# Linear attention through the tokens' Gram matrix instead of keys and values, in a four-layer image network

## The chip, the cores and the metric

The kernel runs on one core of one Trainium2 chip. The metric is the device time of one execution in microseconds; for the kernel before, it is the median of three runs, 8629.55 us (8617.16 to 8655.84). A change of about half a per cent, 43 us, is what such runs can tell from none.

An execution of the kernel before was also recorded by the profiler. Its records name five engines: PE (TensorE, with PEld for its weight loads), DVE (VectorE), ACT (ScalarE), POOL (GpSimd) and SP (SyncE, which here only issues transfers).

## The reference

The input is x of shape (4, 96, 64, 64): four images of 96 channels and 4096 pixels. Four layers follow each other:

- Layer 0: group normalization, a projection, a depthwise convolution and a selective state-space scan in four directions over the 4096 pixels, with a gate and an output projection.
- Layer 1: group normalization and a deformable 3 by 3 convolution (each output pixel gathers nine interpolated input pixels).
- Layer 2: over tokens, a Fourier mixing block, then a feed-forward net in 8-bit arithmetic.
- Layer 3: linear attention, then a second feed-forward net.

The change concerns only the attention. Without its residual it is

```python
qkv = x @ Wqkv + bqkv
q, k, v = jnp.split(qkv, 3, axis=-1)
attn = jnp.einsum('bhnd,bhmd->bhnm', q, k) * D ** (-0.5)
y = jnp.einsum('bhnm,bhmd->bhnd', attn, v)
return y.reshape(B, N, E) @ Wff + bff
```

with 6 heads of 16 channels and x normalized per token (the transposes that move the heads are left out here). There is no softmax, so the order of the products is free: for each head, the sum over all tokens of k times v transposed is a 16 by 16 matrix, and everything behind it is one 97 by 96 matrix that is applied to the tokens.

Written with e, a token with a one appended (97 numbers), keys are Wk'e and values Wv'e, biases included. The sum over tokens of v k' is Wv' (sum of e e') Wk. The sum in brackets is the 97 by 97 Gram matrix of the tokens.

## The kernel before

The whole network is one program. What is placed when is not left to a compiler: a planner writes the instructions of every engine in one order, which each engine then keeps (`in_program_order`).

Three streams of work are merged:

- the scan of layer 0 (`Layer0.scan`), 1536 units of 128 lanes by 1024 steps; it sets the pace;
- the stream `ends`: what comes before the scan for the four images, and layers 2 and 3 (`Layers23.image`), one image after the other;
- the stream `middle`: what follows the scan of an image (`Layer0.behind`), and layer 1 (`Layer1.image`).

Work is written as generators that yield steps with their costs (`cost(pe=..., act=...)`, in us as the planner assumes them). `Clock` keeps the time at which each engine would be free; `has_room` lets a step in if its input is ready and its engines aren't too far ahead of the scan. `pipe` runs several chains of steps side by side, at most `width` at a time, and takes the oldest one that may go. After each scan unit both streams are asked for steps until neither has one that fits; `middle` is asked first (`ends` first in the last image's sampling). So the costs that a step states decide where its instructions and all those after it stand.

`Layers23.image` waits until layer 1 has sampled the image, loads its 96 by 4096 tokens (`t`) by a transfer on SP's queue, and runs the Fourier block, the first feed-forward net, the attention and the second net on it. For the last image nothing is left to lie beside: it is split into two halves of 2048 tokens that run as two streams, with a meeting in the attention, where the sums of both halves are added.

The attention is `LinearAttention.run`. First `normed` makes `tl`, the normalized tokens with a 97th row of ones, channels on partitions (lines 1725 to 1727): `centred` subtracts the mean and gathers the variances, and `spread` (L527) repeats the inverse deviations over partitions. Then come

- `keys_and_values(m)`, for each block of 128 tokens: a matmul of the block with the key and value weights into PSUM (`pk`, L1734), a copy to SBUF by ACT (`kv`, L1736), and a matmul that adds values times keys to `pa` (L1738), three blocks at a time in `pipe` (L1743);
- the product of `pa` with the mask of heads, `vk` (L1748), and for the last image the addition of both halves (L1755);
- two small matmuls with a copy each, `p1` with the output weights (L1759, L1761) and `p2` with the query weights (L1764, L1766), which give the matrix `m2`;
- for each chunk of 512 tokens a matmul with `m2` (`p3`, L1775) and the addition to `t` (L1777).

PSUM is short: the scan has banks of its own, and all other work shares three of them (`net.mm`) until the scan is over; then the stream `ends` gets five more. `net.hold(1)` reserves the one in which `pa` is summed.

Three other places matter for the prediction. L1034 multiplies the scan's input `db`, which PE has spread by L1020, and L1042 scans it. L1295 and L1297 in layer 1 transpose four blocks of 128 pixels on PE and copy them to SBUF. L1112 loads `yta` and `ytc`, layer 0's column results, for `behind`.

Of the kernel before, what the change touches and what calls it, by code (L numbers as in the profile page):

```python
# [8 lines left out]
F32 = mybir.dt.float32  # L9
# [10 lines left out]
B, C, H, W = 4, 96, 64, 64  # L20
# [162 lines left out]
def cost(pe=0.0, dve=0.0, act=0.0, pool=0.0, **more):  # L183
    return Step((pe, dve, act, pool), **more)


def wait(us=0.0, **more):

    return Step((0.0,) * 4, us, **more)
# [82 lines left out]
def pipe(net, chains, width, every=0, lane=None, **tiles):  # L272


    chains, active = iter(chains), []
    clock, known, more = net.clock, net.known, True
    end, free = clock.now(), tiles
    while True:
        if more and len(active) < width:
            steps = next(chains, None)  # L280
            if steps is None:
                more = False
            else:
                active.append(Chain(steps, clock.now()))
                continue
        if not active:
            break
        for n, chain in enumerate(active):
            if chain.new and not net.has_bank():
                continue  # L290
            if any(
                a.done <= chain.done + every
                for a in active[:n]
                if lane is None or (a.kind is lane) == (chain.kind is lane)
            ):
                continue
            if not all(free[tag] > 0 for tag in chain.takes):
                continue
            if clock.has_room(known.get((chain.kind, chain.done), (1.0,) * 4), chain.ready):
                break  # L300
        else:
            yield BLOCKED
            continue
        for tag in chain.takes:
            free[tag] -= 1
        clock.precede(known.get((chain.kind, chain.done), (0.0,) * 4))
        step = next(chain.steps, None)
        if step is None:
            net.hold(-chain.holds)
            active.remove(chain)  # L310
            end = max(end, chain.ready)
            continue
        for tag in step.frees:
            free[tag] += 1
        known[chain.kind, chain.done] = step.work
        chain.ready = clock.queue(step, chain.ready)
        chain.done += 1
        net.hold(step.holds - chain.holds)
        chain.holds, chain.new, chain.takes = step.holds, step.new, step.takes
        yield None  # L320
    yield wait(max(0.0, end - clock.now()))
# [1124 lines left out]
class Fourier:  # L1446
# [77 lines left out]
    def run(self, b, t):  # L1524

        net = self.net
        tc, nc = net.tc, net.nc
        with tc.tile_pool(name=f"l2b{b}", bufs=1) as big:
            tl = big.tile([C + 1, L], F32, name=f"tl{b}", tag="tl")
            nc.gpsimd.memset(tl[C:], 1.0)  # L1530
            with tc.tile_pool(name=f"l2n{b}", bufs=2) as pool:
                yield from normed(net, t, tl, f"2_{b}", pool)
            tv = tl.rearrange("c (n1 n2) -> c n1 n2", n2=64)
            with tc.tile_pool(name=f"l2s{b}", bufs=2) as pool:
                for g in range(2):
                    yield from self.half(f"{b}_{g}", g, tv, t, pool, pool)
# [66 lines left out]
def normed(net, t, tl, key, pool, groups=(0, 1)):  # L1603

    rs = yield from net.centred(
        t, net.cen96, lambda j: (tl[:C, j * CH : (j + 1) * CH], plain), key, pool, groups=groups
    )

    def chain(j):
        cs = slice(j * CH, (j + 1) * CH)  # L1610
        pb = net.spread(rs, 32 * (j % 4) + groups.index(j // 4), C, key)
        yield cost(pe=1.2, holds=1)
        net.nc.vector.tensor_mul(tl[:C, cs], tl[:C, cs], pb)
        yield cost(dve=0.7)

    yield from pipe(net, (chain(j) for j in chunks(groups)), 3)


def chunks(groups):
    return [4 * r + q for r in groups for q in range(4)]  # L1620
# [87 lines left out]
class LinearAttention:  # L1708
# [8 lines left out]
    def run(self, b, t, groups=(0, 1), side="left", shared=None):  # L1717
        net = self.net
        tc, nc = net.tc, net.nc
        key = f"{b}_{groups[0]}"  # L1720
        with (
            tc.tile_pool(name=f"l3b{key}", bufs=1, side=side) as big,
            tc.tile_pool(name=f"l3s{key}", bufs=2, side=side) as pool,
        ):
            tl = big.tile([C + 1, L], F32, name=f"tl3{key}", tag="tl")
            nc.gpsimd.memset(tl[C:], 1.0)
            yield from normed(net, t, tl, f"3_{key}", pool, groups)
            net.hold(1)
            pa = net.mm(f"pa{key}", C)[:, :C]
            blocks = [4 * j + i for j in chunks(groups) for i in range(4)]  # L1730

            def keys_and_values(m):
                pk = net.mm(f"pk{b}_{m}")[:, : 2 * C].rearrange("p (s c) -> p s c", c=C)
                nc.tensor.matmul(pk, lhsT=tl[:, 128 * m : 128 * m + 128], rhs=self.wkv, start=True, stop=True)  # L1734
                kv = pool.tile([128, 2, C], F32, name=f"kv{b}_{m}", tag="kv", bufs=3)
                nc.scalar.copy(kv, pk)  # L1736
                yield cost(pe=0.55, act=0.4)
                nc.tensor.matmul(  # L1738
                    pa, lhsT=kv[:, 1, :], rhs=kv[:, 0, :], start=(m == blocks[0]), stop=(m == blocks[-1])
                )  # L1740
                yield cost(pe=0.4)

            yield from pipe(self.net, (keys_and_values(m) for m in blocks), 3)  # L1743

            if shared is None:
                shared = {}
            vk = shared[groups[0]] = pool.tile([C, C], F32, name=f"vk{key}", tag="vk")
            nc.vector.tensor_mul(vk, pa, self.heads)  # L1748
            net.hold(-1)
            yield cost(dve=0.3)  # L1750
            if len(groups) == 1:
                while len(shared) < 2:
                    yield BLOCKED
                if groups[0] == 0:
                    nc.vector.tensor_add(vk, vk, shared[1])  # L1755
                    yield cost(dve=0.3)
            if groups[0] == 0:
                p1 = net.mm(f"p1{b}", C)[:, :128]
                nc.tensor.matmul(p1, lhsT=vk, rhs=self.wff, start=True, stop=True)  # L1759
                m1 = pool.tile([C, 128], F32, name=f"m1{b}", tag="m1")  # L1760
                nc.scalar.copy(m1, p1)  # L1761
                yield cost(pe=0.6, act=0.3)
                p2 = net.mm(f"p2{b}", C + 1)[:, :128]
                nc.tensor.matmul(p2, lhsT=self.wqT, rhs=m1, start=True, stop=True)  # L1764
                m2 = shared["m2"] = pool.tile([C + 1, 128], F32, name=f"m2{b}", tag="m2")
                nc.scalar.copy(m2, p2)  # L1766
                yield cost(pe=0.6, act=0.3)
            while "m2" not in shared:
                yield BLOCKED
            m2 = shared["m2"]  # L1770

            def chunk(j):
                cs = slice(j * CH, (j + 1) * CH)
                po = net.mm(f"p3{b}_{j}")
                nc.tensor.matmul(po, lhsT=m2, rhs=tl[:, cs], start=True, stop=True)  # L1775
                yield cost(pe=1.0, holds=1)
                nc.vector.scalar_tensor_tensor(t[:, cs], po[:C], net.vec(V_BFF, C), t[:, cs], ALU.add, ALU.add)  # L1777
                yield cost(dve=0.8)

            yield from pipe(self.net, (chunk(j) for j in chunks(groups)), 3)  # L1780
            shared[f"over{groups[0]}"] = True
            while len(groups) == 1 and not ("over0" in shared and "over1" in shared):
                yield BLOCKED
# [137 lines left out]
```

## Time and profile before

| | before |
|---|---|
| median of three runs | 8629.55 us |
| the profiled execution | 8600.48 us |
| its span, first to last instruction | 8598.7 us |
| mean granted clock of TensorE | 0.785 |
| PE busy | 6553.4 us (76%) |
| VectorE busy | 6817.9 us (79%) |
| ScalarE busy | 4945.4 us (58%) |
| GpSimd busy | 5626.7 us (65%) |
| scan of layer 0, first to last unit | 184.9 to 7550.5 us |
| sampling of the last image ends | 8171 us |

The attention's first stage in the four images, by the starts of the first `pk` and the first `vk`:

| image | from, us | to, us | what runs beside it |
|---|---|---|---|
| 0 | 5544.7 | 5642.4 | scan, `behind` |
| 1 | 6877.8 | 6981.6 | scan, sampling of image 2 |
| 2 | 7888.6 | 7929.9 | sampling of image 3 |
| 3 | 8496.4 | 8524.8 | the other half of image 3 |

In a line of the profile's groups stand the line of the program, the engine and operation, output and inputs by name, shapes and count; after the first bar the busy time and the mean duration of one in ns; after the second, how long the engine stood idle just before them and who ended most of that. Shares of busy time are means over stages with different limits. An fp32 matmul shows as two records. In the timeline, lines give start and duration in us, the engine, the line and operation, output from inputs, and in brackets the idle time before. The chain is the chain of work that ended last, followed back from the end. In the waits, each line names who waited, for whom, for how long in total, how often, and the longest.

### The profile page before, as it was taken

What the parts mean: (1) busy time and instruction counts of PE and PEld (TensorE: products, weight loads), DVE (VectorE), ACT (ScalarE), POOL (GpSimd) and SP (SyncE); (2) the same over time, 40 slices, a digit from 0 to 9 for tenths busy, and PEclk for the clock granted to TensorE, in tenths of its full rate; (3) what the DMA queues carried; (4) which work ended last, traced back from release to release, by engine and by line L of the source; (5) the groups of instructions that cost most, each with busy time, mean ns of one, the idle gap of its engine ahead of it and who ended that gap; (6) DMA issues with size and microseconds to landing.
All of it is one profiled execution on the core that took longest, in us unless ns stands there. A gap on an engine that the chain in (4) does not pass through costs nothing.

```text
span 8598.7 us, 97186 instructions
## 1 busy us (share of the span) xinstructions
PE 6553.4 (76%) x31960; PEld 2840.7 (33%) x31960; DVE 6817.9 (79%) x5118; ACT 4945.4 (58%) x9071; POOL 5626.7 (65%) x4308
## 2 busy tenths in 40 slices
PE   6775877689767668777767888777788776897587
PEld 2211221122222223311223555223455331464374
DVE  2799989888799888688898888888887887838714
ACT  5664666556567668755666667554567765333224
POOL 1565667566579788665688888665787886527700
PEclk8766877779677779876777888676788887798698
DMA  3677678868779889876888989766898887744420
GB/s 97 166 198 195 169 196 220 210 166 201 182 216 243 220 230 226 204 193 181 209 228 223 230 230 229 169 163 166 229 228 226 204 216 180 180 104 137 143 63 13
DMA packets 773932, 1608.32 MB, mean 187 GB/s; under 512 B 264081, under 2 KB 355757, under 8 KB 771222
## 3 DMA queue, kind: packets, MB, share of 16 engines
q10 hardware_dynamic: 244224, 843.17, 38.9%
q1 hardware_dynamic: 455478, 532.37, 24.0%
q0 software_dynamic: 73728, 226.57, 10.1%
q8 instruction: 256, 4.19, 0.2%
q14 instruction: 246, 2.02, 0.1%
HBM read 1345.43 MB, written 256.29 MB: 186 GB/s over the span
## 4 chain that ended last, share of the span: by engine, by line
PE 27%; DVE 14%; DMA 7%; ACT 7%; issue 4%; POOL 2%; ACTq 1%; SPq 1%; DVEq 0%; POOLq 0%
DVE hh L1042 7%; DVE db L1034 3%; PE ps L1416 3%; PE f L1510 3%; PE py L1070 3%; DMA da<-de 2%; PE pd L1432 2%; ACT g L1395 2%; PE db L1020 2%; ACT da L1014 1%; PE h L1551 1%; PE yp L1590 1%; PE zp L1576 1%; POOL hh L1051 1%; PE py L1065 1%
## 5 line engine op out<-in xcount | busy, mean ns | idle before, releaser
L1051 POOL TENSOR_TENSOR hh<-hh,bc 128x1024 f32<-128x1024 f32 x1536 | 3672.1, 2393 | 354.9 <-DVE hh L1042 225.1
L1042 DVE TENSOR_TENSOR_SCAN hh<-da,st,db 128x1024 f32<-128x1024 f32 x1152 | 2700.9, 2345 | 209.5 <-PE py L1070 79.8
L1034 DVE TENSOR_TENSOR db<-db,bc 128x1024 f32<-128x1024 f32 x1536 | 1864.0, 1214 | 610.2 <-PE db L1020 608.7
L1014 ACT ACTIVATE da<-da,w_al 128x1024 f32<-128x1024 f32 x1536 | 1737.6, 1146 | 476.8 <-DMA da<-de 129.9
L1383 POOL DMA_INDIRECT g<-table,idx x1152 | 1201.7, 1043 | 372.3 <-issue 174.8
L1020 PE MATMUL db<-du,rep 24*128 24x512 bf16 x3072 | 700.5, 457 | 780.1 <-DVE hh L1042 748.9
L1070 PE MATMUL py<-hh,w_fold 128*32 128x512 f32 x6144 | 1120.5, 792 | 35.4 <-POOL hh L1051 19.3
L1395 ACT ACTIVATE g<-g,wt 128x96 f32<-128x96 f32 x3456 | 968.3, 364 | 116.7 <-PE py L1070 30.7
L1042 DVE TENSOR_TENSOR_SCAN hh<-da,db 128x1024 f32<-128x1024 f32 x384 | 877.2, 2284 | 73.2 <-PE py L1070 25.1
L1416 PE MATMUL ps<-w_ident,g 128*96 128x128 f32 x3744 | 688.8, 329 | 222.8 <-issue 90.6
L1020 PEld LDWEIGHTS <-rep 24*128 24x128 bf16 x3072 | 159.5, 94 | 1909.3 <-issue 1228.5
L851 POOL TENSOR_TENSOR lw<-lw,w 128x512 f32<-128x512 f32 x192 | 244.0, 1271 | 718.0 <-DVE w L849 686.0
L1416 PEld LDWEIGHTS ps<-w_ident,g 128*96 128x96 f32 x3744 | 499.4, 148 | 568.6 <-ACT g L1395 176.7
L1049 POOL COPY st<-hh 128x1 f32<-128x1 f32 x1152 | 235.1, 204 | 685.3 <-DVE hh L1042 650.5
L763 PE MATMUL pc<-pad,wc 96*128 96x512 f32 x1152 | 568.7, 630 | 6.9 <-ACT st L1424 2.6
L1424 ACT COPY st<-ps 96x384 f32<-96x384 f32 x384 | 180.1, 472 | 543.6 <-PE ps L1416 506.0
L882 PE MATMUL pr<-ex,w_ident 128*128 128x512 f32 x384 | 294.7, 859 | 147.6 <-DVE ex L872 58.6
L840 PE MATMUL pd<-xd,w_dtw 103*64 103x512 f32 (+1 forms) x512 | 279.0, 820 | 68.1 <-DVE rl L853 30.4
L1432 PE MATMUL pd<-st,wdc 96*128 96x256 f32 x1152 | 320.5, 430 | 11.4 <-ACT st L1424 4.8
L763 PEld LDWEIGHTS pc<-pad,wc 96*128 96x128 f32 x1152 | 217.1, 199 | 308.7 <-issue 289.2
L1070 PEld LDWEIGHTS py<-hh,w_fold 128*32 128x32 f32 x6144 | 160.5, 125 | 387.4 <-issue 293.6
L1519 ACT COPY d<-f 128x512 f32<-128x512 f32 x192 | 111.2, 581 | 299.7 <-PE f L1510 287.5
(253 smaller groups left out, 8940.0 us busy)
## 6 DMA issues: line engine op xcount, KB each, us to landing
da<-de ACTq DMA_DIRECT2D x1536, 512.0 KB
du<-du SPq DMA_DIRECT2D x1536, 96.0 KB
bc<-bcd SPq DMA_DIRECT2D x128, 512.0 KB
y<-yb SPq DMA_DIRECT2D x384, 128.0 KB
de<-rl SPq DMA_DIRECT2D x128, 256.0 KB
m<-in_dft SPq DMA_DIRECT2D x128, 256.0 KB
ad<-y ACTq DMA_DIRECT2D x192, 128.0 KB
table<-pix SPq DMA_DIRECT2D x256, 96.0 KB
```

The costliest lines, as they stand in the source:

```text
L763: nc.tensor.matmul(pp, lhsT=wc[:, q, g * 128 : (g + 1) * 128], rhs=pad[:, r0 + dy : r0 + dy + NR, dx : dx + W], start=(q == 0), stop=(q == 8),
L882: nc.tensor.matmul(pr, lhsT=net.ident, rhs=ex, start=True, stop=False)
L1014: self.net.nc.scalar.activation(u.da, u.da, AF.Exp, scale=self.al[:, a : a + 1])
L1020: self.net.nc.tensor.matmul(db[:, h, :], lhsT=self.rep[64 * u.q + 32 * h : 64 * u.q + 32 * h + 24], rhs=u.du[64 * u.q + 32 * h : 64 * u.q ...
L1034: self.net.nc.vector.tensor_mul(u.db, u.db, u.bc[:, 0, :])
L1042: nc.vector.tensor_tensor_scan(u.along(u.hh), u.along(u.da), u.along(u.db), first, ALU.mult, ALU.add)
L1051: self.net.nc.gpsimd.tensor_mul(u.hh, u.hh, u.bc[:, 1, :])
L1070: nc.tensor.matmul(py[p0 : p0 + 32], lhsT=self.fold[:, u.i, :], rhs=hc[:, h * CH : (h + 1) * CH], start=u.sums["add"] is None and u.i == 0 ...
L1383: nc.gpsimd.indirect_dma_start(out=g[:, k, :], out_offset=None, in_=self.tables[b % 2], in_offset=bass.IndirectOffsetOnAxis(ap=idx[:, n : ...
L1395: nc.scalar.activation(pixel, pixel, AF.Identity, scale=wt[:, n, c : c + 1])
L1416: nc.tensor.matmul(pt[:, k, :], lhsT=g[:, k, c * C : (c + 1) * C], rhs=net.ident, is_transpose=True, start=(c == 0), stop=(c == corners - 1),)
L1432: nc.tensor.matmul(po, lhsT=wdc[:, k, :], rhs=st[:, k, :], start=(k == 0), stop=(k == 8))
```

## The change

Keys and values are not made. `gram(j)` takes a chunk of 512 tokens: four transposes on PE turn 97 by 128 blocks of `tl` into 128 by 97, ACT copies them to SBUF in one instruction, and four matmuls add each block's product with itself to `pg`, 97 by 97. There are 8 such chunks in an image, three at a time in `pipe`, with two steps each, where there were 32 blocks with two steps. The steps state their own costs.

After the sum, the Gram matrix is copied from PSUM to SBUF (`sums`), and the halves of the last image are added as before, now as 97 by 97. Two matmuls then apply the key weights (`pk`, copied by ACT to `gk`) and the value weights (`pa`), and the mask of heads is applied to the second one. Everything from `p1` on is as it was.

```diff
             net.hold(1)
-            pa = net.mm(f"pa{key}", C)[:, :C]
-            blocks = [4 * j + i for j in chunks(groups) for i in range(4)]
-
-            def keys_and_values(m):
-                pk = net.mm(f"pk{b}_{m}")[:, : 2 * C].rearrange("p (s c) -> p s c", c=C)
-                nc.tensor.matmul(pk, lhsT=tl[:, 128 * m : 128 * m + 128], rhs=self.wkv, start=True, stop=True)
-                kv = pool.tile([128, 2, C], F32, name=f"kv{b}_{m}", tag="kv", bufs=3)
-                nc.scalar.copy(kv, pk)
-                yield cost(pe=0.55, act=0.4)
-                nc.tensor.matmul(
-                    pa, lhsT=kv[:, 1, :], rhs=kv[:, 0, :], start=(m == blocks[0]), stop=(m == blocks[-1])
-                )
-                yield cost(pe=0.4)
-
-            yield from pipe(self.net, (keys_and_values(m) for m in blocks), 3)
+            pg = net.mm(f"pg{key}", C + 1)[:, : C + 1]
+            js = chunks(groups)
+
+            def gram(j):
+                pt = net.mm(f"pt3{b}_{j}")[:, : 4 * (C + 1)].rearrange("p (q c) -> p q c", c=C + 1)
+                for q in range(4):
+                    m = 4 * j + q
+                    nc.tensor.transpose(
+                        pt[:, q, :], tl[:, 128 * m : 128 * m + 128], net.ident[: C + 1, : C + 1]
+                    )
+                xt = pool.tile([128, 4, C + 1], F32, name=f"xt{b}_{j}", tag="xt", bufs=3)
+                nc.scalar.copy(xt, pt)
+                yield cost(pe=0.8, act=0.6)
+                for q in range(4):
+                    nc.tensor.matmul(
+                        pg,
+                        lhsT=xt[:, q, :],
+                        rhs=xt[:, q, :],
+                        start=(j == js[0] and q == 0),
+                        stop=(j == js[-1] and q == 3),
+                    )
+                yield cost(pe=1.4)
+
+            yield from pipe(self.net, (gram(j) for j in js), 3)
 
             if shared is None:
                 shared = {}
-            vk = shared[groups[0]] = pool.tile([C, C], F32, name=f"vk{key}", tag="vk")
-            nc.vector.tensor_mul(vk, pa, self.heads)
+            sums = shared[groups[0]] = pool.tile([C + 1, C + 1], F32, name=f"gr{key}", tag="gr")
+            nc.vector.tensor_copy(sums, pg)
             net.hold(-1)
             yield cost(dve=0.3)
             if len(groups) == 1:
                 while len(shared) < 2:
                     yield BLOCKED
                 if groups[0] == 0:
-                    nc.vector.tensor_add(vk, vk, shared[1])
+                    nc.vector.tensor_add(sums, sums, shared[1])
                     yield cost(dve=0.3)
+            if groups[0] == 0:
+                pk = net.mm(f"pk{b}", C + 1)[:, :C]
+                nc.tensor.matmul(pk, lhsT=sums, rhs=self.wkv[:, :C], start=True, stop=True)
+                gk = pool.tile([C + 1, C], F32, name=f"gk{b}", tag="gk")
+                nc.scalar.copy(gk, pk)
+                yield cost(pe=0.6, act=0.3)
+                pa = net.mm(f"pa{b}", C)[:, :C]
+                nc.tensor.matmul(pa, lhsT=self.wkv[:, C:], rhs=gk, start=True, stop=True)
+                vk = pool.tile([C, C], F32, name=f"vk{b}", tag="vk")
+                nc.vector.tensor_mul(vk, pa, self.heads)
+                yield cost(pe=0.6, dve=0.3)
             if groups[0] == 0:
                 p1 = net.mm(f"p1{b}", C)[:, :128]
                 nc.tensor.matmul(p1, lhsT=vk, rhs=self.wff, start=True, stop=True)
```

## The prediction

> **What bounds the kernel now.** I read the page first, its busy slices and its groups of instructions, then the chain that ended last in order of time, then the waits of single stretches. The groups show what the scan of layer 0 waits for:
>
> ```profile
> L1042 DVE TENSOR_TENSOR_SCAN hh<-da,st,db 128x1024 f32<-128x1024 f32 x1152 | 2700.9, 2345 | 209.5 <-PE py L1070 79.8
> L1034 DVE TENSOR_TENSOR db<-db,bc 128x1024 f32<-128x1024 f32 x1536 | 1864.0, 1214 | 610.2 <-PE db L1020 608.7
> ```
>
> The 1536 scans run from 184.9 to 7550.5 us: 4.80 us each, of which VectorE itself needs 2.35 + 1.21. In the rest stands the work that the planner lays beside the scan, and 609 us in which VectorE waits for PE to get round to db. So PE work beside the scan is not free, but VectorE leads. After the scan comes a serial end; these are pieces of the chain in order of time:
>
> ```profile
> 7414.34 24.09 DMA ytc<-y
> ...
> 8165.32 5.32 PE pd L1432 x18
> 8172.96 8.79 DMA t<-x
> ...
> 8527.11 10.19 PE p L1775 x16
> ```
>
> Image 3 is sampled until 8171 us, then its tokens are loaded, and layers 2 and 3 of it run alone to 8598.7. Only there is the attention certainly on the path: from the first pk at 8496.4 to vk at 8525.1, 28.7 us, with PE busy 27.8 of 31 us. One steady period of it, two blocks of 128 tokens:
>
> ```profile
> 8513.67 0.63 PEld L1734 LDWEIGHTS pk<-w_wkv,tl 97*128 97x128 f32 x4
> 8513.75 0.84 PE L1734 MATMUL pk<-w_wkv,tl 97*128 97x192 f32 x4
> 8514.30 0.70 ACT L1736 COPY kv<-pk 128x192 f32<-128x192 f32 x2 [0.85 <-PE pk L1734]
> 8514.67 0.63 PEld L1738 LDWEIGHTS pa<-kv 128*96 128x96 f32 x4 [0.38 <-ACT kv L1736]
> 8514.67 0.79 PE L1738 MATMUL pa<-kv 128*96 128x96 f32 x4
> 8515.22 0.63 PEld L1734 LDWEIGHTS pk<-w_wkv,tl 97*128 97x128 f32 x4
> ```
>
> The period is 1.55 us: 1.0 us from pk to pa, 0.38 of it waiting for the copy, then 0.55 for pa. The transposes that are added have a near twin in layer 1, line 1295, here at full clock:
>
> ```profile
> 7697.95 0.42 PEld L1295 LDWEIGHTS pt<-w_ident,x 96*128 96x128 f32 x4
> 7698.06 0.50 PE L1295 MATMUL pt<-w_ident,x 96*128 96x96 f32 x4
> 7698.31 0.97 PEld L1300 LDWEIGHTS pm<-w_add,oc 128*128 128x128 f32 x8
> 7698.64 0.47 ACT L1297 COPY pix<-pt 128x384 f32<-128x384 f32 x1
> ```
>
> Four transposes hold PE's load queue 0.36 us, and their copy takes 0.47 us.
>
> **What the Trainium skill says.** "FP8 and Floating Point Precision", section TensorE Precision Notes: a true fp32 product takes four passes through the array. The trace fits: each fp32 matmul here has two records, and one of 512 columns takes 2 x 0.43 us. "TensorE: Matmul & The Clock Gate", section Terms, has a transpose mode that is four times faster for fp32; here a transpose has one record against a matmul's two, at 0.09 us for 96 columns. The same page, section LDWEIGHTS, lets a load grow with the columns loaded; 128 columns take 0.19 us and 96 take 0.16 as the records count them. "Perfetto Trace Analysis", section Tensor Engine Instruction, says that the end of a matmul is estimated; so I price from start to start.
>
> **The change, part by part.** Per image the old stage has 32 blocks: 64 records each of pk and pa, and 32 copies of 0.318 us. In the last stretch that is 16 periods of 1.55 = 24.8 us; the rest of the 28.7 is the other half's spreading (8 records at 0.43 = 3.4) and ends.
>
> (a) New, per chunk of four blocks: four transposes, 0.36 us; one copy of 128x388, 0.48; four Gram products of 97x97, eight records like pa's, twice 0.55 = 1.1. PE 1.46 us, if the copy is hidden, against two periods, 3.1. The planner takes the oldest chain whose input is ready; with three open chains and a copy between the two steps it comes out as two chunks transposed, then two summed. The first copy starts 0.69 us after its transposes and ends at 1.16, so the first Gram product starts at about 1.3, when two chunks of transposes (0.72) are long over: 0.55 lost per pair. A pair takes 1.3 + 2.2 = 3.5, a chunk 1.75. For eight chunks: (3.1 - 1.75) x 8 = 10.8 gained; 13 with all copies hidden, 5.6 if each chunk waits for its own (1.3 + 1.1 = 2.4). I take 11.
>
> What is late next: the other half's spreading needs lns, done at 8503.1, and it sat in PE's queue until 8508.2. With half 0 summed at 8503.5 it can start at once, so the gain is not eaten by that wait, with nothing left over.
>
> (b) sums <- pg is a copy of 97x97 where the 96x96 product with heads was, 0.25 us; the addition of both halves stays. Then two more legs in series before p1: pk with its copy, pa with its product with heads. The two old legs of this form run start to start 8525.40, 8526.21, 8527.11: 0.81 and 0.90. So +1.7 us on the path, as nothing else is left for PE there. The end: -11 + 1.7 = -9.3.
>
> (c) Image 2 (7888.6 to 7929.9) lies beside the sampling of image 3. There POOL issues 13 to 15 gathers in each 20 us, with and without image 2 (whose result is stored from 8030 on, while sampling ends at 8171). Its gain is worth 0; if sampling bent to it, at most 1 to 2 us.
>
> (d) Images 0 and 1 lie beside the scan: 5544.7 to 5642.4 and 6877.8 to 6981.6. PE records 39.3 and 29.2 us busy in them; by the ratio 1.46 to 2.36 (0.63 and 0.55 per two blocks, so 2.36 in four) about 26 us of both go. ACT loses 2 x (9.8 - 4.1) = 11 us. VectorE, which leads, loses nothing, and the Gram steps are longer (1.1 us at full clock, 1.5 at 0.75) in front of db in PE's queue, where single steps had 0.3 to 0.5. VectorE waits for db 609 of 7366 us while PE is about 80% busy; a tenth to a third of the PE time freed comes back: 3 to 9 us. I take -5. Bounds: -15 and +10.
>
> (e) These stages also shorten. Before, 64 steps took 98 us, three in each scan unit; now it is 16 steps, and two more in series at 4 to 5 us each: about 35 + 10 us. The stream of layers 2 and 3 is 50 us ahead after image 0 and 100 after image 1. At the end of image 1, 7223, that runs into a wait: image 2 isn't sampled before 7204, so it starts 20 to 30 us earlier and no more. But that place stalls the scan now; of the waits from 7195 to 7300:
>
> ```profile
> DVE db L1034 <- PE db L1020: 37.5, 5, 29.1
> PEld lnc L485 <- DMA t<-x: 30.3, 1, 30.3
> SPq L1805 <- DMA out<-t: 6.9, 1, 6.9
> ```
>
> The first centring of image 2 stands at the head of PE's queue and waits 30 us for its tokens, which wait on SP for the store of image 1 and share the engines with the load of yta and ytc. Behind it db waits, and no scan starts for 29 us. With image 1 stored at about 7120, the load follows yta directly: stall about 20. I take -8; bounds -20 and +30 (it lands behind the whole of yta and ytc, 24 us in the chain). The other handover, 5850 (12.9 us of db's wait), moves to about 5800 and stays as it is: 0.
>
> Sum, against the profiled execution of 8600.5 us (span 8598.7): -9.3 - 5 - 8 = -22, so 8578. The median of the runs shown, 8629.55, lies 29 us above that profile; I apply the difference to it: **8607.5**, or -0.26%. Half a per cent, 43 us, is about what this kernel's runs (8617 to 8656) can tell from no change.
>
> **The rivals.**
> *The end alone.* Beside the scan nothing is won: db's wait comes from other work, and the handover stalls as before. For it: VectorE's own work there is unchanged. Against: PE is the releaser of nearly all of db's wait. -9: 8620.
> *The order moves favourably.* From 7550 to 7720 PE is busy 152 of 170 us with image 2's Fourier products while offsets and positions of image 3, which set the end, queue behind them. If image 2 is 30 us further by then, and the scan no later, most of that comes off the path: -22 - 30 = -52, so 8578. Against: the Fourier work moves to beside the scan and slows it there.
> *Slower: a worse handover.* If both token loads (5800 and 7204) land behind a load of yta and ytc, each stall becomes 30 + 24 = 54 us, instead of 29 and 13: +25 and +41, with -14 from the end and (d): +52, so 8681. It decides from about 57 us of added stall, which takes both. For it: SP issues in program order, and the middle stream steps first. Against: at 5800 no yta load stands near; the scan stalls of 5400 to 5500 are over.
> That the change computes something else can be left out: the Gram matrix includes the row of ones, hence the biases.
>
> **How the numbers follow.** Forecast 0.45, the end alone 0.25, favourable 0.18, slower 0.08, and 0.04 for reorderings that I can't name, half on each side. The likeliest has its own range of 8590 to 8630. The range for 8 in 10 runs from 8562 to 8652: most of the favourable case below, and above the end alone with (d) at +10 and (e) at +22. Faster by over 0.5% (below 8586): 0.20. Within: 0.70. Slower (above 8673): 0.10.
>
> **What the profile of the changed kernel would show.** (a) Four transposes start to start with the next load in 0.36 to 0.45 us, copies of 0.48, sums of four blocks in 1.0 to 1.2; the last image's stage, first transpose to sums added, 17 to 20 us instead of 28.7. (b) 1.6 to 2.0 us more from that to the first p3. (c) Sampling of image 3 at the same 13 to 15 gathers in 20 us. (d) Under 60 us for the stage of images 0 and 1, and db's wait a little below 609. (e) Image 2's tokens loaded at about 7205, the wait of lnc at about 20. From the sampling's end to the end of the span, 427 us before, 418. The prediction is wrong if the scan's end moves by over 30 us from 7550, through stalls at handovers, or if the Gram step holds PE at 2.4 us a chunk.

## The result and the profile after

The changed kernel takes 8589.89 us (median of 8 runs, 8555.16 to 8620.80) beside 8645.10 us of the kernel before (8 runs, 8617.16 to 8655.84): a ratio of 0.9940, 95% interval 0.9920 to 0.9959. That is 55 us less, 0.6%. A second measurement (below, e11) gave 0.9928, 0.9900 to 0.9955. The forecast was 22 us less.

The two groups of the scan, in the profile of the kernel after (busy time and mean of one in ns; then VectorE's idle time before them and its releasers):

```profile
L1042 DVE TENSOR_TENSOR_SCAN hh<-da,st,db 128x1024 f32<-128x1024 f32 x1152 | 2701.3, 2345 | 205.3 <-PE py L1070 68.5
L1034 DVE TENSOR_TENSOR db<-db,bc 128x1024 f32<-128x1024 f32 x1536 | 1863.1, 1213 | 561.7 <-PE db L1020 542.2
```

VectorE's own work is what it was; its idle time before db fell from 610.2 to 561.7 us, and the part of it that PE ended from 608.7 to 542.2. The scan ends at 7489.4 us instead of 7550.6, and the end is 10 us shorter. Single traces scatter: in a second trace of each order (e1 and e11 below) the scan ends at 7521.7 and 7495.5, so the means lie 44 us apart and not 61.

The end, in the timeline of the kernel after (start, duration, engine, line; in brackets the idle time before):

```profile
8490.75 0.89 PE L1736 MATMUL pt<-w_ident,tl 97*128 97x97 f32 x8
8491.34 0.87 ACT L1740 COPY xt<-pt 128x388 f32<-128x388 f32 x2 [1.15 <-PE pt L1736]
8491.88 1.61 PE L1743 MATMUL pg<-xt 128*97 128x97 f32 x16 [0.24 <-ACT xt L1740]
8493.25 0.73 PEld L1736 LDWEIGHTS pt<-w_ident,tl 97*128 97x128 f32 x8
8493.33 0.83 PE L1736 MATMUL pt<-w_ident,tl 97*128 97x97 f32 x8
...
8498.77 3.67 PE L527 MATMUL lnb<-lns,w_ident 128*128 128x512 f32 x8 [2.75 <-DVE lns L436]
...
8507.81 0.26 DVE L1764 TENSOR_TENSOR gr<-gr,gr 97x97 f32<-97x97 f32 x1
...
8508.86 0.41 PE L1773 MATMUL pa<-gk,w_wkv 97*96 97x96 f32 x2 [0.33 <-ACT gk L1770]
...
8511.36 1.22 PE L1795 MATMUL p<-tl,m 97*128 97x512 f32 x1 [0.35 <-ACT m L1786]
```

Two chunks are transposed, then two are summed, and the pair takes 8493.25 - 8490.75 = 2.5 us where the forecast had 3.5. A copy of a chunk has a median of 0.48 us. Between the halves PE stands idle for 2.75 us, since the inverse deviations of the other half (`lns`) aren't ready; only then comes its spreading. From the first transpose to the added sums it is 17.3 us, where the old stage had 28.7; from there to the first p3 3.3 us, where vk had 2.0.

The chain of work that ended last, in order of time (start, duration, what):

```profile
7158.47 8.70 SPq L1112
7167.21 13.50 DMA t<-x
...
8054.76 11.35 another core or an unknown queue
8167.16 8.75 DMA t<-x
...
8511.36 10.15 PE p L1795 x16
```

The tokens of image 2 now load directly behind the load of yta, at 7167.2, and those of image 3 at 8167.2, only 6 us before those of the kernel before, although the scan ended 61 us before. The sampling of image 3 took 500 us in this execution, from its first gather to the load of the tokens, and 449 in the kernel before. The chain puts 44.5 us of this stretch, in eight pieces (the longest, 11.35 us, is shown), down to another core or an unknown queue; in the other 13 traces it puts nothing there. What that was stays open. In a second trace of the same kernel the sampling takes 457 us, so the 50 us belonged to that one execution, and its span of 8582.9 us tells too little of the gain.

The handover from image 1 to 2, waits from 7130 to 7230 us of the kernel after (who waited, for whom, total, times, longest):

```profile
DVE db L1034 <- PE db L1020: 37.3, 5, 22.3
PEld lnc L485 <- issue: 27.3, 7, 23.3
PE lnc L485 <- DMA t<-x: 23.0, 1, 23.0
```

PE's wait for the tokens went from 30.3 to 23.0 us, as forecast. VectorE's wait for db behind it hardly followed: 37.3 us, 37.5 before (32.8 and 37.8 in the second traces, e11 and e1).

### The profile page after: what moved, and what is told of

Same layout as the page of the kernel before. It is cut to its first block, busy times and chain, and to the rows that moved or that the text cites. A ratio compares the mean times of both kernels' runs of the same rounds, so it can differ in the third digit from the quotient of the medians.

```text
span 8582.9 us, 96776 instructions
## 1 busy us (share of the span) xinstructions
PE 6491.0 (76%) x31814; PEld 2822.5 (33%) x31848; DVE 6815.3 (79%) x5122; ACT 4923.9 (57%) x8979; POOL 5616.1 (65%) x4308
## 4 chain that ended last, share of the span: by engine, by line
PE 35%; DVE 30%; DMA 9%; issue 9%; ACT 9%; POOL 4%; SPq 1%; ACTq 1%; another core or an unknown queue 1%; DVEq 0%; POOLq 0%
DVE hh L1042 15%; DVE db L1034 8%; PE pc L763 4%; PE py L1070 4%; PE ps L1416 3%; PE f L1510 3%; POOL hh L1051 3%; ACT g L1395 2%; PE pd L1432 2%; PE db L1020 2%; DMA da<-de 2%; ACT da L1014 2%; PE h L1551 1%; PE zp L1576 1%; DMA m<-in_dft 1%
## 5 line engine op out<-in xcount | busy, mean ns | idle before, releaser
L1042 DVE TENSOR_TENSOR_SCAN hh<-da,st,db 128x1024 f32<-128x1024 f32 x1152 | 2701.3, 2345 | 205.3 <-PE py L1070 68.5
L1034 DVE TENSOR_TENSOR db<-db,bc 128x1024 f32<-128x1024 f32 x1536 | 1863.1, 1213 | 561.7 <-PE db L1020 542.2
L1432 PE MATMUL pd<-st,wdc 96*128 96x256 f32 x1152 | 323.0, 434 | 11.6 <-ACT st L1424 4.2
```

Source lines behind the costliest of these rows:

```text
L1034: self.net.nc.vector.tensor_mul(u.db, u.db, u.bc[:, 0, :])
L1042: nc.vector.tensor_tensor_scan(u.along(u.hh), u.along(u.da), u.along(u.db), first, ALU.mult, ALU.add)
L1432: nc.tensor.matmul(po, lhsT=wdc[:, k, :], rhs=st[:, k, :], start=(k == 0), stop=(k == 8))
```

## The experiments

Five terms add up to a span: what comes before unit 1090 of the scan's 1536 (up to there the order of the work is the same in all kernels but those with longer landing times, e6, e7, e9 and e12); units 1090 to the end; from there to the first gather of image 3; its sampling, up to the load of its tokens; the end. In us, from one trace of each:

| kernel | to unit 1090 | units 1090 to end | to first gather | sampling | end |
|---|---|---|---|---|---|
| before | 5440 | 2111 | 173 | 449 | 426 |
| e1, Gram in image 3 only | 5425 | 2097 | 173 | 459 | 420 |
| after | 5435 | 2055 | 178 | 500 | 416 |
| e11, after again | 5444 | 2051 | 177 | 457 | 416 |
| e2, Gram in images 0 and 1 only | 5442 | 2071 | 179 | 454 | 427 |
| e5, after with four times the transposes | 5441 | 2059 | 177 | 454 | 416 |
| e3, after, images held back | 5438 | 2039 | 184 | 452 | 413 |
| e6, after, longer landing times | 5424 | 2013 | 223 | 454 | 415 |
| e12, e6 again | 5448 | 2005 | 224 | 451 | 418 |
| e10, after, shifted by 12 us | 5448 | 2024 | 165 | 451 | 416 |
| e4, before, lower stated costs | 5457 | 2061 | 169 | 446 | 426 |
| e7, before, longer landing times | 5416 | 2033 | 190 | 452 | 423 |
| e8, before, shifted by 12 us | 5414 | 2072 | 183 | 450 | 426 |
| e9, before, longer wait for tokens | 5420 | 2039 | 180 | 465 | 426 |

The first column differs by up to 44 us between kernels with the same order up to there, and by 24 us between e6 and e12, which are the same program: that is how far one execution differs from another. In the second, orders that agree stay together: before and e1 at 2111 and 2097; after, e11, e2 and e5 between 2051 and 2071; e6 and e12 at 2013 and 2005.

And the times, each beside the kernel before on the same chip (its medians there: 8600.5 for e1 to e4, 8605.9 for e5 to e8, 8601.5 for e9 to e12). The ratios are not the quotients of these medians and differ from them by up to 0.0017:

| kernel | median, us | ratio to before | 95% interval |
|---|---|---|---|
| e1 | 8601.3 | 1.0005 | 0.9991 to 1.0020 |
| e2 | 8561.4 | 0.9951 | 0.9936 to 0.9967 |
| e3 | 8529.8 | 0.9935 | 0.9909 to 0.9961 |
| e4 | 8552.1 | 0.9945 | 0.9924 to 0.9967 |
| e5 | 8549.6 | 0.9942 | 0.9918 to 0.9966 |
| e6 | 8532.5 | 0.9919 | 0.9890 to 0.9948 |
| e7 | 8542.8 | 0.9933 | 0.9911 to 0.9955 |
| e8 | 8579.9 | 0.9968 | 0.9954 to 0.9982 |
| e9 | 8547.0 | 0.9938 | 0.9917 to 0.9958 |
| e10 | 8484.7 | 0.9866 | 0.9840 to 0.9891 |
| e11 | 8546.2 | 0.9928 | 0.9900 to 0.9955 |
| e12 | 8520.6 | 0.9908 | 0.9888 to 0.9928 |

### The end and the scan apart: e1 and e2

Both keep both forms of the attention and choose by image.

```diff
+        made = self.by_gram if b in (3,) else self.by_keys        # e1
+        made = self.by_gram if b in (0, 1) else self.by_keys      # e2
+        yield from made(b, t, groups, side, shared)
```

> The Gram matrix in the last image alone; images 0 to 2 make keys and values as before. Nothing before the last image's attention changes its place, so its trace up to 8165 us is also a second look at the kernel before. All theories agree: the stage from the first instruction of the sum to the added sums takes 17 us instead of 28.7, the legs behind it 1.7 more, the end from the last sampling to the end of the span 418 instead of 427; in time 10 us less than before (0.1%). If the whole gain of 55 us were in the end, it would be 55 here.

> The Gram matrix in images 0 and 1 alone, beside the scan; images 2 and 3 as before. Both theories of a shorter scan (less work on PE; the stream of layers 2 and 3 earlier) expect the scan to end 50 to 60 us earlier, at about 7490, and 35 to 50 us less in time. The theory that only the end gains expects no difference.

Measured: 1.0005 and 0.9951. The end's 10 us don't show in the total of e1 (the interval begins at -0.09%, and 10 us are 0.12%), though its trace has an end of 420 us instead of 426; the granted clock, below, may have hidden them. Most of the gain, 0.49% of 0.6 to 0.7, comes with images 0 and 1. The scan of e2 ends at 7513.7, not at about 7490 as expected. The end itself is told better by the traces: it lasts 416.3 us in the mean of the eight traces with the Gram form in image 3, and 425.6 in the six others. That is -9.3.

### Is it the stream's lead: e3 and e4

With shorter stages, image 0 is stored at 5762.7 instead of 5849.6 and image 1 at 7129.0 instead of 7223.7. e3 takes that lead back, by waits in the planner's reckoning after each sum; e4 keeps keys and values and states lower costs for their steps, so that the planner packs them closer.

```diff
+HELD = (48.0, 45.0)
...
+            if b < 2:
+                yield wait(HELD[b])                                # e3
...
-                yield cost(pe=0.55, act=0.4)
+                yield cost(pe=0.2, act=0.15) if b < 2 else cost(pe=0.55, act=0.4)   # e4
-                yield cost(pe=0.4)
+                yield cost(pe=0.35) if b < 2 else cost(pe=0.4)
```

> The changed kernel, but in images 0 and 1 the planner is told to wait 48 and 45 us after the sum, so that the stream of layers 2 and 3 comes to about the places it had before, with the new, smaller work. If the smaller work on PE shortens the scan: scan ends 40 us or more before 7550, time 45 to 55 us less than before. If the earlier place of the stream does it: the scan ends within 20 us of 7550, and only the end's 10 us are left, with at most 15 for the work.

> The kernel before, with keys and values everywhere, but the steps of that stage state in images 0 and 1 the smaller costs of the Gram steps (2.2 us of PE for four blocks instead of 3.8), so that the planner lays the old work closer together and the stream comes earlier. If the earlier place brings the gain: the stage of image 0 shrinks from 98 us to 60 or less, and the scan ends 30 to 45 us earlier. If the smaller work brings it: no difference, or up to 15 us more, as the same work now crowds in front of the scan's db.

Measured: e3 stores image 0 at 5830.7 and image 1 at 7242.8, so most of the lead is gone in the first and all of it in the second. The gain is still there, 0.9935, as it was expected for the smaller work. So the lead isn't needed for the gain. e4 did not bring a lead at all (image 0 stored at 5858.4), so it can't test one; but it gained as much, 0.9945, with the old attention's whole work. This was the first sign that the order alone can do it, without the new attention.

### Is it PE's load: e5

The changed kernel, with each transpose of images 0 and 1 made four times. The stated costs stay, and so does what is computed.

```diff
-                for q in range(4):
+                for q in [0, 1, 2, 3] * (4 if b < 2 else 1):
```

> The changed kernel with the same order and the same stated costs, but in images 0 and 1 each chunk's four transposes are made four times over (the same values each time), which brings PE's work of a chunk from about 1.46 us to 2.5, the level of keys and values (2.36). If less work on PE shortens the scan, the 13 us that the changed kernel won in units 1112 to 1135, beside image 0's sum, are lost again, and about 15 to 20 us in all. If only the order counts, the time is that of the changed kernel, within 5 us.

Transposes on PE in the kernel after and in e5 (count; shortest, median and longest in ns):

```profile
L1736 PE MATMUL pt<-w_ident,tl x128: 244/247/424, 5539.2 to 8505.4; 97*128 97x97 f32 x128
```

```profile
L1736 PE MATMUL pt<-w_ident,tl x320: 244/247/422, 5546.8 to 8470.3; 97*128 97x97 f32 x160
```

The count at the very end of the second line is that of a sample; 320 is the whole. 192 more transposes at a pitch of 0.09 us are 17 us of PE. The records of the stage in images 0 and 1 add up to 68.5 us of PE in the kernel before (39.3 + 29.2), 25.9 in the kernel after and 43.5 in e5, so e5 puts back about two fifths of what the change freed. In the traces, the instructions stand in the same order on every engine, the repeated transposes apart.

Measured: 0.9942, beside 0.9940 and 0.9928 for the changed kernel. If 50 us had come from PE being free, some 20 should have gone. The interval, 0.9918 to 0.9966, can't exclude that alone, but the trace speaks against it: the second column has 2059 for e5, within the 2051 to 2071 of the same order, and units 1112 to 1135, beside image 0's sum, keep their gain (104.6 us; 101.9 and 104.8 in the two traces of the changed kernel, 116.2 and 114.5 in the two of the old order). So the gain as a whole is not PE's load. A gain of some 5 us, as forecast, can't be told by this.

### Is it the order: e6, e7, e8 and e9

The planner takes it that a load has landed 4 us after its issue. In the traces, PE and VectorE stand 10 to 30 us at the head of their queues before a load's arrival. e6 (on the changed kernel) and e7 (on the kernel before) give four loads longer times. e9 gives it to the tokens alone. e8 only shifts the plan: 12 us of waiting in the planner's reckoning, after image 0's keys and values; nothing on the chip waits by it.

```diff
-                    yield wait(4.0)      # yta and ytc, L1114
+                    yield wait(24.0)     # e6, e7
-            yield wait(4.0)              # x1, L1251
+            yield wait(24.0)             # e6, e7
-            yield wait(4.0)              # sampling bases, L1321
+            yield wait(18.0)             # e6, e7
-            yield wait(4.0)              # tokens
+            yield wait(24.0)             # e6, e7, e9
...
+            if b == 0:
+                yield wait(12.0)         # e8
```

> The changed kernel with four assumed landing times of transfers raised in the planner, from 4 us to 24 (tokens of layers 2 and 3, layer 1's image, yta and ytc) and 18 (base): the planner then puts what needs the data behind 20 us more of other work. If instructions that stand at the head of an engine's queue and wait for such transfers stall the scan, the stalls of over 11 us between two scans (68 us in the changed kernel's trace, units 1090 to 1535) fall below 30, and the time by 30 us or more. If those stalls only take the place of other waits, no difference.

> The kernel before, attention unchanged, with the same four raised landing times. If the changed kernel's gain beside the scan comes from fewer stalls at transfers, this one wins 30 to 50 us as well, without any smaller work, and its stalls of over 11 us fall from 82 to below 40. If the gain comes from the smaller work, it wins less than 10.

> The kernel before, with one step of 12 us of waiting told to the planner after image 0's keys and values; no work differs. It tells what a mere shift of the order by some three scan units is worth. If the order that a plan happens to fall into moves the time by tens of us, this differs from before by 0.2% or more in either direction; if it takes less work or an earlier stream, it stays within 0.15%.

> The kernel before, with the planner told that an image's tokens land 24 us after their load is issued and not 4 (one number; the attention keeps its keys and values). If the stalls at the two handovers of images are what the plan of before lost (16.6 us at 5860 and 32.8 us at 7216 in its trace), those two shrink to under 10 and 20 us while the 24.6 us stall at 6051, which waits for the sampling bases, stays: 25 to 35 us less, 8565 to 8575 beside a kernel before at 8600. If the gain comes from the order as a whole, whichever wait it is that moves it, the time falls by 20 to 55 us and the stall at 6051 goes or moves as well. If the old attention's amount of work is the cause, nothing: within 15 us of the kernel before.

Measured: all three with the old attention gain, e7 0.9933, e8 0.9968, e9 0.9938; e6 gains 0.9919. One number in the plan (e9) is worth about as much as the change. It did more than its place. The stalls of the scan at the handovers (a stall is the time from one scan's start to the next, 4.8 us in the mean, where it is over 11) shrank from 16.6 to 12.3 us at the first and from 32.8 to 16.2 and 11.6 at the second; but so did one that has nothing to do with tokens, from 24.6 to 14.7. What the stalls from unit 1090 on have over 4.7 us each sums to 81.8 us in the kernel before and to 27.7 in e7, below the 40 that was expected; in e6 it is 50.2, and not below 30. Waits of the kernel before, 6020 to 6080 us:

```profile
DVE pos L1334 <- DMA da<-de: 15.9, 1, 15.9
ACT da L1014 <- DVE ind L1356: 11.8, 1, 11.8
POOL st L1049 <- DVE hh L1042: 11.6, 8, 3.1
ACT d L1519 <- PE f L1510: 11.5, 6, 6.3
ACT L1330 <- DMA table<-pix: 9.9, 1, 9.9
```

The positions of image 2 stand at the head of VectorE's queue and wait 15.9 us (the trace names another transfer; by the program it is the load of the sampling bases, which SP issues at 6060.4, behind the stores of the table). ScalarE waits 9.9 us for the table beside it. The next scan starts 24.6 us after the one before. The same place in e9, 5985 to 6045:

```profile
DVE pos L1334 <- DMA da<-de: 5.9, 1, 5.9
```

and in the kernel after, 5990 to 6050, where no wait of `pos` is left among the larger ones:

```profile
DVE db L1034 <- PE db L1020: 8.3, 3, 5.6
```

Units 1190 to 1230, which hold this place, take 199.8 and 198.3 us in the two traces of the old order (before, e1), and 176.0, 176.1, 176.5 and 175.9 in the four of the changed one (after, e2, e5, e11). These 23 us are the largest piece of the change's gain, at a place where no attention runs (image 0's first stage ends before unit 1135, image 1's begins behind 1390). That piece belongs to the order: with e4's order the same units take 180 us with the old attention, with e6's 197 with the new one. It is more than the wait of `pos`, though: in e4's trace that wait is still 11.6 us.

A second piece goes with the form. Units 1390 to 1465, which hold image 1's attention and what follows it, take 305 to 323 us in all kernels with the Gram form there but e3, which holds that work back (331); with keys and values they take 326 to 338 in all six traces. Units 1112 to 1190, the same for image 0, don't part like that: 354 to 396 against 372 to 398.

### How far the order goes: e10, e11 and e12

e10 puts e8's 12 us into the changed kernel, after image 0's sum. e11 is the changed kernel, e12 is e6, both without any edit and on one chip.

> The changed kernel, with a wait of 12 us in the planner's reckoning after the Gram sum of image 0, which does nothing on the chip but move the order of what follows. If the Gram form itself is worth 50 us beside the scan, the ratio stays within 0.2 per cent of the changed kernel's (0.992 to 0.996). If the gain is that of one lucky order, a shift of 12 us draws another one: the ratio lands anywhere from 0.990 to 1.001, and the summed stalls above 11 us of the scan's second half, 67.6 us in the changed kernel's trace, move by over 15 us.

> The changed kernel unchanged, beside the version below on one chip. A second trace of it: the sampling of image 3, 498 us from its first gather to the last sampled row in the first trace, is 445 to 458 as in every other trace, if those 50 us belonged to that one execution; the scan ends 50 to 70 us before 7550, since the order is the same. Ratio to the kernel before 0.991 to 0.997.

> The changed kernel with the planner's landing times at 24, 24, 18 and 24 us, unchanged from its first run (ratio 0.9919 there), now beside the changed kernel on the same chip. If the longer landing times add to the change, it is 10 to 35 us faster than the changed kernel. If both only replace one unfavourable order, the two agree within 10 us.

Measured on that chip: the changed kernel 8546.2, e12 8520.6, e10 8484.7 us. By the medians e12 is 26 us faster than the changed kernel and e10 61 us. The intervals of e12 and e11 overlap, so the 26 us aren't sure; those of e10 and e11 don't. Both again beat the kernel before. e10's ratio, 0.9866, lies even outside the span that was expected for a lucky order. e11 shows sampling at 456 us (to the last sampled row, as in the expectation) and the scan's end at 7495.5, as expected.

e10's summed stalls are 76 us, 80.2 and 67.6 in the two traces of the changed kernel: here the expectation missed. What fell is the rest, the intervals of up to 11 us: 4.37 us a unit where the changed kernel has 4.42 and 4.46, and the old order 4.55 and 4.51. So in the changed kernel, too, most of the gain lies in many short intervals and not in the long stalls. Indeed e10 has the worst handover of all; its waits from 7090 to 7200 us:

```profile
DVE db L1034 <- PE db L1020: 33.0, 3, 30.0
PE lnc L485 <- DMA t<-x: 29.6, 1, 29.6
```

The fastest of all these kernels keeps the 30 us stall that the forecast wanted shortened, and e9, whose waits there (7160 to 7270 us) are small, is slower by 62 us:

```profile
DVE db L1034 <- PE db L1020: 12.0, 5, 3.7
```

Neither is an earlier end of the scan a gain as such: e6 and e12 need some 45 us less for it than the changed kernel, but 223 us from there to the first gather instead of 177. What isn't done beside the scan is done behind it.

**The granted clock.** TensorE's granted clock is not the same in all runs: its means on this chip are 0.7845 in the kernel before, 0.7867 in e11, 0.7890 in e9 and 0.7912 in e10. In the 87 runs of the kernel before on the three chips, a clock higher by 0.01 goes with a time shorter by 53 us. An estimate with this slope puts 12 us of e11's gain, 24 of e9's and 36 of e10's down to the clock. The lead of e10 over the changed kernel, 51 us between the means, would then be 27, and the smallest of the gains from e2 to e12 would be 25 (e8). e1 ran at 0.7834 beside 0.7850, which is worth 8 us the other way, about what was missing of its end. Whether the clock is a cause here, or follows from the order of the work, no run shows.

**The form's own part.** With the same edit to the plan, the Gram form is the faster one each time: 0.994 against 1 with none, 0.992 and 0.991 against 0.993 with longer landing times (where the intervals overlap), 0.987 against 0.997 with the shift; 0.001 of that is the end. Taken over orders, units 1090 to the end last 2033 us in the mean of four with the Gram form (2009 to 2059, the traces of one order averaged first) and 2062 in that of five with keys and values (2033 to 2104). The orders of either scatter by more than the 29 us between them. But the 29 us can be placed. Units 1112 to 1135 and 1390 to 1465, beside the attention of images 0 and 1, take together 407 to 428 us in the eight traces with the Gram form and 438 to 461 in the six others, 417 and 446 in the means over orders. All other units from 1090 on take 1616 and 1615 in these means, and there the orders scatter from 1593 to 1655. So the form has its part beside the scan, where the attention is. The stretches were chosen with the traces known; no run was made to test them. For the change itself (two traces of the old order, four of the new) 24 us come off in these stretches, 21 in the other units, where the order is what differs, and 9 in the end.

**What stays open.** Not settled is what makes the 24 us: fewer steps, less work on ScalarE or PE, or a stream that is through earlier. e5 takes 428 us in these stretches, the other three traces of its order 423 to 424, so the time of the transposes on PE is, as far as one trace tells, a small part; no run took the others apart.

## Why the prediction was right or wrong

The range, 8562 to 8652, held the time of 8589.9. The sign was right, and the size too small: 22 us were forecast and 55 came. The absolute time came out nearer than the gain by chance: the kernel before took 8645 us beside it, and not the 8629.55 that the forecast started from. The sign, too, owes something to chance, since about 21 of the 55 us came from an order that the forecast hadn't priced.

**(a) and (b), the end: right, for a reason and for a chance.** -9.3 forecast, -9.3 between the means of the traces. The two legs cost 3.3 - 2.0 = 1.3 us (1.7 forecast; 1.6 to 2.0 in the list of what would show). The stage is 17.3 us, in the span of 17 to 20. Inside, two errors cancel: a chunk takes 1.25 us, not 1.75, as the transposes and products of a pair overlap more than I took; and "with nothing left over" was wrong, since PE then waits 2.75 us for `lns`, which VectorE finishes at about 8498.6.

**(c), image 2 beside the sampling: right.** Its stage fell to 22 us, and the sampling lasts 446 to 465 us with keys and values in image 2, 451 to 457 with the Gram form, if the one execution with 500 is left out. Nothing is gained. (The gathers come at 10 to 15 in 20 us in e11; counted in the same way, they came at 11 to 16 before, not 13 to 15.)

**(d), less work on PE: the signs came, the size failed, and the cause isn't shown.** The stages of images 0 and 1 took 47 and 35 us to the sum, and 53 and 46 to vk, below 60, and PE's part of db's wait fell to 542. But that is 66 us less (51 between the means of two traces of each order), where I had the scan gain 5, and the PE time freed was 43 us, not 26. Beside the attention the scan gained 24 us, and with two fifths of the PE time put back in e5 nearly all of that is still there. That PE is the releaser of db's wait doesn't mean that PE's load is what is waited for: PE comes late to db also because an instruction at the head of its queue, or of VectorE's, waits for something else.

**(e), the handover from image 1 to 2: the step that failed.** The load moved up behind that of yta, and PE's wait for it fell to 23.0 us (about 20 in the forecast). It came at 7167.2, not at 7205, as the scan was further by then. I had turned the shorter wait into 8 us of scan. VectorE's wait there hardly moved (37.5 and 37.8 us in the two traces of the old order, 37.3 and 32.8 in those of the new), and e10 shows that a stall of 30 us at this place goes with the best time. The handover of image 0, put at 0, moved from 16.6 to 12.1 us.

**What was missing: the plan.** The forecast let each step stay where it was and priced it there. But the number of steps and their stated costs changed, so everything behind image 0 was planned anew. What that is worth can be seen on the old attention, where e4, e7, e8 and e9 change the plan alone: 0.3 to 0.7%, 26 to 63 us. I had given "reorderings that I can't name" 0.04. By the forecast's own test, "wrong if the scan's end moves by over 30 us from 7550", the mechanism was wrong: it moved by 61, and by 55 in the second trace. The test named stalls at handovers; the largest piece went at the positions of image 2 instead. The favourable rival had the size (-52) and not the place: the stretch from the scan's end to the first gather, from which Fourier work was to leave, went from 173 to 178 us. "The end alone" fell with e2; the worse handover never came.

The order that the kernel before had was itself a poor one: the four others that were tried with the same attention (e4, e7, e8, e9) are all faster, by 0.3 to 0.7%.

## What to carry to other kernels

Where a planner places the instructions, a change to one stage re-deals everything behind it: before believing a gain of under one per cent, shift the plan of the old kernel by a harmless amount and see how far that alone moves the time. Here one shift moved it by 0.3%, and other stated times by 0.5 to 0.7%, as much as the whole change; and shifted plans are a cheaper search than a new stage (e10, one more wait in the plan, took 61 us more off the median, part of which may be the clock). What the stage itself is worth showed only when the stretches beside it were compared over several plans. A wait with a name, PE for the tokens or VectorE for PE, is not yet time that can be won: what counts is when the next thing in the chain starts, and the same 30 us stood in the slowest plan and in the fastest.

## What the runs showed that I had not expected

- One execution of the changed kernel sampled image 3 in 500 us, where the same kernel took 457 in another and all other kernels between 446 and 465. A single trace can carry 50 us that no other shows; it was seen only by cutting the span into its terms.
- The same 1.5 MB load of tokens takes 8.75 us where nothing else moves (8167.2 in the chain) and 13.5 us directly behind the load of yta and ytc (7167.2), where PE, which asked early, waited 23.0. Counted from the issue, the planner's 4 us were short by a factor of 2 to 3.4.
- Until unit 1090, where the order is the same, traces of this program drift apart by up to 44 us (5414 to 5457), nearly as much as the whole change.
